# Two gate products of a four-layer convolution kernel, each as one 128x128 product, with sums, bias and relu on VectorE

## The chip, the core and the metric

The kernel runs on one core of a Trainium2 chip. The metric is the device time of one execution in microseconds. The kernel before took 975.81 us (median of three executions, 974.52 to 977.21). A difference under about 0.3%, 2.9 us, can't be told from none.

The core has a matrix engine (TensorE, PE in the profile, with its weight loads as PEld), a vector engine (VectorE, DVE), a scalar engine (ScalarE, ACT), GpSimd (POOL) and SyncE (SP), which issues most transfers. Each works through its own list of instructions in order and waits on semaphores of the others.

## The reference, cut to what matters

Sixteen images of 256 channels, 28 x 28, go through four layers. Layer 1 is the one concerned. It has two branches, each with a gate per image and channel:

```python
def se_gate(mix, w1, b1, w2, b2):
    p = mix.mean(axis=(2, 3))                  # 256 means
    h = jax.nn.relu(p @ w1.T + b1)             # 32 hidden values
    g = jax.nn.sigmoid(h @ w2.T + b2)          # 256 gates
    return g[:, :, None, None]
...
y = prelu(bn(conv3x3(hardsign(x + a_move), a_w), a_bn1), a_alpha2)
mix = s * x + y * (1.0 - s)
y = se_gate(mix, a_se_w1, a_se_b1, a_se_w2, a_se_b2) * y
y = y * residual
y = bn(y, a_bn2) + residual
res2 = y
u = prelu(bn(conv1x1(hardsign(y + f_move), f_w), f_bn1), f_alpha2)
mix2 = s2 * y + (1.0 - s2) * u
u = se_gate(mix2, f_se_w1, f_se_b1, f_se_w2, f_se_b2) * u
return bn(u, f_bn2) + res2
```

So a branch has a product of 256 means with 32 rows, and one of 32 hidden values with 256 rows.

## The kernel before, in words

Layer 0 takes the first 115 us, layer 1 lasts to 479 us, layer 2 to 690 us and layer 3, an attention, to the end.

**An image of layer 1.** Channels lie on 128 partitions in two halves (k for input channels, mo for output channels). `iteration(b)` runs the 3x3 convolution of image b beside the first branch's gate of image b-1 and the second branch's gate of image b-2, so the two gates of one `iteration` share each small product: two columns, one for each branch (g = 0, 1). PE does, in this order: `conv_pair(b, 0, ...)` for parts 1 and 2, then part 0; the product for the hidden sums; part 3; the product for the gates; `conv_pair(b, 1, ...)` for parts 1 and 2, then 0 and 3; and `conv1x1(b - 1)`. That is 96 and 16 matmuls of 392 columns. Their results go to PSUM buffers of `conv_ps`, three of them, six allocations in an image. A buffer is free when its last reader has finished.

**Order by hand.** Layer 1 stands in a `manual_schedule` over PE, DVE and Activation: on these three engines the instructions run in the order of the program text.

**VectorE in an image,** in this order: `enter` (L669) and `prelu_y` (L765) of the next and last image, `unit_b` (L765), three small operations for the means (`hidden_x`, `hidden_a`, L134), `sum_pair_b` (L744), `residual_b` (L705), `transform` (L134, into vs), `residual_b` again, `rows_out` (L753), the product of gates and s_bn (L134 in `gates`), `transform`, `branch1_b` twice (L808), `prelu_y`, `branch2` (L845), `sum_pair_b`, `branch2`, `transform` twice, `rows_out`.

**ScalarE in an image:** `unit_u` (L836), `sign1` (L675), `sum_pair_a` (L734), `residual_a` (L663), `sign1`, the relu in `hidden_b` (L784), `residual_a`, the sigmoid in `gates` (L793), `branch1_a` twice (L801), `widen` (L695), `branch1_c` (L815), `sum_pair_a`, `branch1_c`, `widen`, `squares2` twice (L854), weight passes of layer 2 in images 1 to 12 (L266, L285, L288; L266 in images 1 to 6 only), `widen` twice.

**The gates.** `hidden_sums` (L619) multiplies the means p, 128 x (g, k), with w_1, 128 x (k, 128): two matmuls, k = 0 and 1, add up in PSUM. Of w_1's 128 columns, 32 for each g are filled; the rest is zero. `hidden_b` (L780) adds the bias b_1 and takes the relu with one ScalarE activation for each g, from 32 partitions of PSUM into `hidden`, whose rows 64 and 96 hold a one that brings in the second bias through w_2's rows. `gates` (L787) multiplies w_2, one half mo after the other, takes the sigmoid from PSUM on ScalarE and multiplies with s_bn on VectorE. `gate_bias` (L626) is called in image 0 alone: it adds a constant part of the mean to b_1.

**After the last image** (L990 to L1060) the same functions run twice more in the open: for the last image's first gate, and for its second, whose gate enters the statistics that layer 2's normalization starts from. `keep_busy` puts matmuls without use on PE there. Between the second `hidden_a` and `gates`, program order has `squares2` on ScalarE, `hidden_b`, two `products` (L857) on VectorE, a `squares` (L854), five small VectorE operations, `gates` and another `squares`.

**Loading.** `constants` (L547) works out the small vectors in layer 0 and issues the loads of w_1, w_2 and b_1 on SP. `vec` holds all per-channel vectors, named in `VECS`; `pv` picks one.

Of the kernel before, what the change touches and what calls it, by code (L numbers as in the profile page):

```python
# [27 lines left out]
F32 = mybir.dt.float32  # L28
# [5 lines left out]
AF = mybir.ActivationFunctionType  # L34
ALU = mybir.AluOpType
# [4 lines left out]
P = 128  # L40
# [29 lines left out]
    + [f"a_bn1_{i}" for i in range(4)] + [f"a_bn2_{i}" for i in range(4)]  # L70
    + ["a_scale", "f_move", "f_alpha2"]
    + [f"f_bn1_{i}" for i in range(4)] + [f"f_bn2_{i}" for i in range(4)]
    + ["f_scale", "g1", "b1", "g2", "b2", "g3", "b3", "a1", "a2", "a3"]
)


def conv_seq_kernel(tc: tile.TileContext, d: dict, out: bass.AP):
    again = forward(tc, d, out, False)
    with tc.If(again > 0):
        forward(tc, d, out, True)  # L80
# [3 lines left out]
def forward(ctx: ExitStack, tc: tile.TileContext, d: dict, out: bass.AP, careful: bool):  # L84
# [3 lines left out]
    nc = tc.nc  # L88
    V, A, T = nc.vector, nc.scalar, nc.tensor
# [3 lines left out]
    small = ctx.enter_context(tc.tile_pool(name="small", bufs=3))  # L93
# [7 lines left out]
    def pv(name):  # L101
        return vec[:, VECS.index(name), :]
# [30 lines left out]
    def tt(o, a, b, op):  # L133
        V.tensor_tensor(o, a, b, op)  # L134
        return o

    def rsqrt(name, v, half=None):

        r, t = (const.tile(list(v.shape), F32, name=name + q) for q in ("_r", "_t"))
        A.activation(t, v, AF.Sqrt)  # L140
        V.reciprocal(r, t)
        tt(t, r, r, ALU.mult)
        if half is not None:
            tt(r, r, half, ALU.mult)
        else:
            V.tensor_scalar(r, r, -0.5, None, ALU.mult)
        tt(t, t, v, ALU.mult)
        V.scalar_tensor_tensor(r, t, -3.0, r, ALU.add, ALU.mult)
        return r
# [270 lines left out]
    with tc.tile_pool(name="ps_conv", bufs=3, space=PSUM) as psc, \  # L420
# [13 lines left out]
        with tc.tile_pool(name="ph1", bufs=1) as ph:  # L434
# [104 lines left out]
            ra1, ra2, rf2, us1, ns1 = (vtile(q) for q in ("ra1", "ra2", "rf2", "us1", "ns1"))  # L539
            mix_x, mix_y, mix_c = (const.tile([P, 2, 2], F32, name=n) for n in ("mix_x", "mix_y", "mix_c"))  # L540

            w_1, w_2, b_1 = (ph.tile(sh, F32, name=n) for sh, n in (([P, 2, P], "se1"), ([P, 256], "se2"), ([64, 1], "seb")))

            for t in (w_1, w_2):
                nc.gpsimd.memset(t, 0.0)

            def constants():  # L547
                for p in pads:
                    nc.gpsimd.memset(p, 0.0)
                nc.gpsimd.tensor_copy(  # L550
                    doubts[:, 4 * NB:4 * NB + 6], vec[:, VECS.index("a1"):VECS.index("a3") + 1, :].rearrange("p i k -> p (i k)")
                )
                for i, n in enumerate(("a_alpha2", "f_alpha2")):
                    nc.gpsimd.tensor_copy(doubts[:, 4 * NB + 6 + 2 * i:4 * NB + 8 + 2 * i], pv(n))
                v = const.tile([P, 4, 2], F32, name="v_bn")
                for i, bn in enumerate(bns):
                    V.tensor_scalar(v[:, 2 * i:2 * i + 2], bn[:, 3::4], EPS, None, ALU.add)
                r = rsqrt("bn", v)
                for i, bn in enumerate(bns):
                    two = slice(2 * i, 2 * i + 2)  # L560
                    tt(s_bn[:, two], bn[:, 0::4], r[:, two], ALU.mult)
                    tt(c_bn[:, two], bn[:, 2::4], s_bn[:, two], ALU.mult)
                    tt(c_bn[:, two], bn[:, 1::4], c_bn[:, two], ALU.subtract)
                tt(cc, c2, c4, ALU.add)

                for o, q in ((ra1, "a_alpha1"), (ra2, "a_alpha2"), (rf2, "f_alpha2")):
                    V.tensor_scalar(o, pv(q), -1.0, 1.0, ALU.mult, ALU.add)
                V.tensor_scalar(us1, s1, 1.0 / UP, None, ALU.mult)
                V.tensor_scalar(ns1, s1, -1.0 / UP, None, ALU.mult)
                tt(zb2, c2, pv("f_move"), ALU.add)  # L570
                for g, (q, scale) in enumerate((("a", pv("a_scale")), ("f", pv("f_scale")))):
                    V.tensor_scalar(mix_x[:, g], scale, 1.0 / N, None, ALU.mult)
                    V.tensor_scalar(mix_y[:, g], scale, -1.0 / N, 1.0 / N, ALU.mult, ALU.add)
                    rows = slice(32 * g, 32 * g + 32)
                    nc.sync.dma_start(out=w_1[:, :, rows], in_=d[f"se1_{q}"])
                    nc.sync.dma_start(out=w_2[rows], in_=d[f"se2_{q}"])
                    nc.sync.dma_start(out=b_1[rows], in_=d[f"seb_{q}"])
                    nc.sync.dma_start(out=w_2[64 + 32 * g:65 + 32 * g], in_=d[f"seb2_{q}"])
                tt(mix_c[:, 1], pv("f_scale"), c2, ALU.mult)

            w2a = packed_weights(wpool, tag="wa2")
# [28 lines left out]

            hidden = [ph.tile([P, 2], F32, name=f"hidden{i}") for i in range(3)]
            for t in hidden:
                nc.gpsimd.memset(t, 0.0)
                for g in range(2):
                    nc.gpsimd.memset(t[64 + 32 * g:65 + 32 * g, g:g + 1], 1.0)

            def hidden_sums(p):  # L619

                ps = pss.tile([P, 2], F32, tag="sm", name="hid")
                for k in range(2):
                    T.matmul(ps, lhsT=w_1[:, k, :], rhs=p[:, :, k], start=(k == 0), stop=(k == 1))
                return [ps[32 * g:32 * g + 32, g:g + 1] for g in range(2)]

            def gate_bias():  # L626
                for g, h in enumerate(hidden_sums(mix_c)):
                    rows = slice(32 * g, 32 * g + 32)
                    tt(b_1[rows], h, b_1[rows], ALU.add)

            vs = ph.tile([P, 2, 4, 2, HR, S + 2], FR, tag="vs", name="vs")
            vs16 = vs if careful else ph.tile([P, 2, 4, 2, HR, S + 2], BF16, name="vs16")
# [9 lines left out]
            sums = {}  # L642
# [131 lines left out]
            def hidden_a(t, p):  # L774

                r = small.tile([P, 2, 2], F32, tag="g1", name="g1")
                tt(r, sums_of(t)[1], mix_y, ALU.mult)
                return hidden_sums(tt(p, p, r, ALU.add))

            def hidden_b(t, sums):  # L780
                h = hidden[t % 3]
                for g, ps in enumerate(sums):
                    rows = slice(32 * g, 32 * g + 32)
                    A.activation(h[rows, g:g + 1], ps, AF.Relu, bias=b_1[rows])  # L784
                return h

            def gates(h, f=None):  # L787

                ps = pss.tile([P, 2, 2], F32, tag="sm", name="gate")
                g = small.tile([P, 2, 2], F32, tag="gate", name="gates")  # L790
                for k in range(2):
                    T.matmul(ps[:, k], lhsT=w_2[:, k * P:(k + 1) * P], rhs=h, start=True, stop=True)
                A.activation(g.rearrange("p i k -> p k i"), ps, AF.Sigmoid)  # L793
                if f is not None:
                    return tt(f, g[:, 1], s_bn[:, 3], ALU.mult)
                return tt(g, g, s_bn[:, 1::2], ALU.mult)
# [69 lines left out]
            def iteration(b):  # L866
# [29 lines left out]
                if one:  # L896
                    h = hidden_b(b, h)
# [7 lines left out]
                if one:  # L905
                    g = gates(h)
                else:
                    gate_bias()
# [57 lines left out]
            with tc.manual_schedule(engines={ET.PE, ET.DVE, ET.Activation}):  # L966
# [24 lines left out]
                b = B - 1  # L991
                keep_busy(14)
                g = gates(hidden_b(B, hidden_a(B, px)))
                keep_busy(14)
                branch1_a(b, 1, g[:, 0])
# [33 lines left out]
                h = hidden_a(B + 1, px)  # L1029
                for k in range(2):  # L1030
                    squares2(b - 1, k)
                h = hidden_b(B + 1, h)
                for k in range(2):
                    products(x2[b][:, k, :], shift[:, k:k + 1], us[b, k], sum_uv[:, k:k + 1])
# [4 lines left out]
                tt(v1, v1, sum_vv, ALU.add)  # L1039
                V.tensor_scalar(v1, v1, 1.0 / (B * N), EPS, ALU.mult, ALU.add)  # L1040
                g = gates(h, dqg[:, 2])
                squares(us[b, 1], 0.0, sum_uu[:, 1:2], (B * N)**-0.5)
                keep_busy(14)
# [712 lines left out]
```

## Time and profile before

The profiled execution took 975.5 us; its span from first to last instruction is 973.7 us, at a granted TensorE clock of 0.994.

| from the page and the stretches | value |
|---|---|
| median of three executions | 975.81 us |
| profiled execution, its span | 975.5 us, 973.7 us |
| PE, VectorE, ScalarE busy over the span | 97%, 79%, 74% |
| 130 to 459 us (16 images): PE, VectorE, ScalarE busy | 328.15, 285.18, 265.84 of 329 us |
| 459 to 480 us: the same | 19.21, 17.17, 14.21 of 21 us |
| L623 hidden sums: matmul records, mean | 64 in images 1 to 15, 230 ns |
| L792 gates: the same | 64, 232 ns |
| L784 relu on ScalarE | 32, 252 ns |

A line of a timeline gives start, duration, engine, line of the program, operation, output<-input with shapes, and, in brackets, how long the engine had been idle and what ended it. Several equal instructions in a row are merged (x2). A matmul of 32-bit floats appears as two records. A busy PE is not a PE at its peak, but an engine that never waits sets the pace of its stretch. An operation that also sums up (L669, L765, L808, L845) has a second record of 0.08 us.

### The profile page before, as it was taken

To read this page: it belongs to the slowest core of one execution; us is meant where nothing else is said; L and a number is where in the kernel's file an instruction comes from. 1 tells how busy PE (TensorE), PEld (TensorE's weight loads), DVE (VectorE), ACT (ScalarE), POOL (GpSimd) and SP (SyncE) were. 2 spreads that over 40 slices of the span, in tenths; PEclk is the share of its full clock that TensorE was granted. 3 is DMA by queue.
4 is the path that set the end of the run, shared out by engine and by line. 5 is a ranking of instruction groups with operands and counts; after the bars stand their busy time and mean duration, and the time that the engine had idled before them with its cause. 6 is when DMAs were issued, how large, how long until landed. Compare 5 with 4: busy or idle time off the path is not lost.

```text
span 973.7 us, 14804 instructions
## 1 busy us (share of the span) xinstructions
PE 944.8 (97%) x5615; PEld 582.8 (60%) x5615; DVE 773.4 (79%) x1417; ACT 722.3 (74%) x1199; POOL 141.0 (14%) x149
## 2 busy tenths in 40 slices
PE   7999899999999999999999999999999999999996
PEld 3555568877887878887555555555444444444443
DVE  4767878899998889985799997999757777777765
ACT  6787468888888888874788868887676767666652
POOL 3000100000000000000100000000054444444431
PEclk9999999999999999999999999999999999999998
DMA  9877513334443222110490000000044353525212
GB/s 347 312 271 270 197 50 99 116 115 131 146 152 117 100 100 96 58 63 34 180 383 1 1 1 1 1 1 1 1 71 96 72 129 70 130 67 133 67 67 103
DMA packets 26948, 105.82 MB, mean 109 GB/s; under 512 B 3490, under 2 KB 7268, under 8 KB 26868
## 3 DMA queue, kind: packets, MB, share of 16 engines
q1 hardware_dynamic: 20948, 73.44, 21.2%
q0 software_dynamic: 5632, 30.54, 11.6%
q8 instruction: 46, 0.75, 0.3%
q10 hardware_dynamic: 288, 0.80, 0.2%
q14 instruction: 34, 0.28, 0.1%
HBM read 72.67 MB, written 32.11 MB: 108 GB/s over the span
## 4 chain that ended last, share of the span: by engine, by line
PE 46%; DVE 3%; ACT 1%; issue 1%; DVEq 0%; ACTq 0%
PE cv L340 19%; PE sc L1331 8%; PE av L1352 8%; PE mi L1308 4%; PE sm L1394 2%; PE mi L1412 2%; PE sm L1352 1%; DVE p L1118 1%; DVE ab L354 0%; ACT es L1335 0%; DVE l2b_fin L1120 0%; DVE l2c_fin L1120 0%; DVE r L1378 0%; DVE p L1295 0%; PE sc L1412 0%
## 5 line engine op out<-in xcount | busy, mean ns | idle before, releaser
L340 PE MATMUL cv<-fpads,wpk 128*128 128x392 f16 (+1 forms) x1746 | 295.7, 331 | 10.2 <-ACT fpads L451 5.0
L713 PE MATMUL cv<-vs,w 128*128 128x392 bf16 (+1 forms) x1536 | 287.1, 356 | 2.9 <-DVE vs L134 2.7
L340 PEld LDWEIGHTS <-wpk 128*128 128x128 f16 x1746 | 169.0, 97 | 137.3 <-issue 9.9
L713 PEld LDWEIGHTS cv<-vs,w 128*128 128x128 f32 x768 | 142.6, 190 | 11.7 <-ACT vs L695 0.7
L1335 ACT ACTIVATE es<-sc 128x784 f32<-128x784 f32 x112 | 87.3, 822 | 41.4 <-PE sc L1331 41.4
L713 PEld LDWEIGHTS <-w 128*128 128x128 f16 x768 | 67.7, 101 | 58.1 <-issue 18.5
L1331 PE MATMUL sc<-q,keyswa 64*128 64x392 f32 x448 | 89.9, 513 | 0.9 <-ACT es L1335 0.9
L1118 DVE SCALAR_TENSOR_TENSOR p<-ab,vec 128x392 f32<-128x392 f32 x128 | 79.1, 618 | 2.3
L1352 PE MATMUL av<-es,v 128*64 128x392 f32 x448 | 80.7, 499 | 0.0
L1345 POOL TENSOR_TENSOR sum<-sum,es 128x784 f32<-128x784 f32 x32 | 67.2, 2100 | 3.1 <-ACT es L1335 0.6
L1331 PEld LDWEIGHTS sc<-q,keyswa 64*128 64x128 f32 x448 | 38.9, 186 | 44.0 <-issue 17.1
L851 POOL DMA_DIRECT2D x2d<-x x16 | 8.6, 537 | 343.9 <-DVE x L845 280.9
L1319 DVE COPY keyswa<-mi 64x392 f32<-64x392 f32 x31 | 16.3, 564 | 52.6 <-ACT q L1315 52.5
L1352 PEld LDWEIGHTS av<-es,v 128*64 128x64 f32 x448 | 29.4, 136 | 47.4 <-issue 47.0
L695 ACT CAST vs<-vs 128x840 fp32r<-128x840 bf16 x64 | 54.7, 882 | 1.5 <-DVE vs L134 1.5
L351 ACT ACTIVATE t<-cv,rounding 128x392 f32<-128x392 f32 (+2 forms) x82 | 51.6, 630 | 4.9 <-PE cv L340 1.9
L1123 ACT ACTIVATE t<-ab 128x392 f32<-128x392 f32 x64 | 33.5, 524 | 27.9 <-DVE ab L354 27.9
L823 PE MATMUL cv<-z,fw 128*128 128x392 f32 x256 | 48.9, 342 | 1.0 <-ACT z L815 0.8
L354 DVE SCALAR_TENSOR_TENSOR ab<-ab,cv 128x392 f32<-128x392 f32 x64 | 35.5, 554 | 17.5 <-ACT ab L352 17.5
L823 PEld LDWEIGHTS cv<-z,fw 128*128 128x128 f32 x256 | 45.7, 188 | 2.3 <-ACT z L815 2.1
L1308 PE MATMUL mi<-p,wqk 128*128 128x392 f32 x124 | 45.3, 506 | 0.3 <-DVE p L1295 0.3
L432 PE MATMUL unused<-idle 128*128 128x512 bf16 x175 | 40.5, 389 | 3.0 <-POOL idle L468 3.0
(287 smaller groups left out, 1511.4 us busy)
## 6 DMA issues: line engine op xcount, KB each, us to landing
xs<-in_x_dram SPq DMA_DIRECT2D x30, 784.0 KB, 5.8
x2d<-x POOLq DMA_DIRECT2D x16, 784.0 KB, 3.8
out_dram<-p SPq DMA_DIRECT2D x15, 784.0 KB, 3.8
p<-x2d POOLq DMA_DIRECT2D x14, 784.0 KB, 6.9
p<-x2d SPq DMA_DIRECT2D x13, 784.0 KB, 16.1
n0d<-n POOLq DMA_DIRECT2D x16, 392.0 KB, 4.7
n<-n0d SPq DMA_DIRECT2D x16, 392.0 KB, 3.3
st<-in_w_dram SPq DMA_DIRECT2D x12, 384.0 KB, 6.1
```

The lines of the kernel that those rows point to most:

```text
L340: T.matmul(pss[j][:, n // size if careful else h, :rows * S].rearrange("p (a b) -> p a b", b=S), lhsT=w[:, n, t, :], rhs=pads[:, blocks[j] ...
L351: A.activation(by_halves(t, blocks[j]), ps, AF.Identity, bias=rounding, scale=1.0 / PACK)
L432: tc.keep_in_program_order(T.matmul(ps, lhsT=idle[:, 0:P], rhs=idle, start=True, stop=True))
L695: A.copy(v, w)
L713: T.matmul(ps.rearrange("p (a b) -> p a b", b=S), lhsT=w[:, k, c, u, mo * P:(mo + 1) * P], rhs=v[:, b % 2, u, k, :, c:c + S], start=(n == ...
L823: T.matmul(ps[:, h, :HN], lhsT=w[:, k, mo * P:(mo + 1) * P], rhs=z2[b][:, k, h * HN:(h + 1) * HN], start=(k + i == 0), stop=(k + i == 2),)
L1118: V.scalar_tensor_tensor(p, y, alpha[:, mo:mo + 1], y, ALU.mult, ALU.max)
L1308: T.matmul(ps[:, h, :HN], lhsT=wqk[:, k, :], rhs=x[b][:, k, h * HN:(h + 1) * HN], start=(k == 0), stop=(k == 1))
L1331: T.matmul(ps[:, h, :HN], lhsT=chunk[rows], rhs=qs[b][rows], start=True, stop=True)
L1335: A.activation(e, ps[:, :, :HN], AF.Exp, scale=0.125)
L1345: (V if late else nc.gpsimd).tensor_tensor(sums[b, late], sums[b, late], e, ALU.add)
L1352: T.matmul(ps[64 * h:64 * h + 64, :HN], lhsT=w, rhs=e[:, h, :], start=start, stop=stop)
```

## The change

Both halves k of the means go through one product: w_1 becomes 128 x 128, with 64 columns for k = 0 and 64 for k = 1, and the right side has four columns (g, k). What is wanted are partitions 0 to 63 in columns k = 0 and partitions 64 to 127 in columns k = 1; VectorE adds these two. Both halves mo of the gates also go through one product: w_2 becomes 128 x 128, with 64 rows for each mo, and `hidden` gets four columns (mo, g), in each of which 32 rows are filled. The relu moves to VectorE; the second bias is no longer a row of w_2 but a vector b_2 that VectorE adds ahead of the sigmoid.

```diff
-            w_1, w_2, b_1 = (ph.tile(sh, F32, name=n) for sh, n in (([P, 2, P], "se1"), ([P, 256], "se2"), ([64, 1], "seb")))
-
-            for t in (w_1, w_2):
-                nc.gpsimd.memset(t, 0.0)
+            w_1, w_2, b_1, b_2 = (
+                ph.tile(sh, F32, name=n)
+                for sh, n in (([P, 2, 64], "se1"), ([P, P], "se2"), ([P, 1], "seb"), ([P, 2, 2], "seb2"))
+            )
...
                     nc.sync.dma_start(out=w_1[:, :, rows], in_=d[f"se1_{q}"])
-                    nc.sync.dma_start(out=w_2[rows], in_=d[f"se2_{q}"])
-                    nc.sync.dma_start(out=b_1[rows], in_=d[f"seb_{q}"])
-                    nc.sync.dma_start(out=w_2[64 + 32 * g:65 + 32 * g], in_=d[f"seb2_{q}"])
+                    for mo in range(2):
+                        nc.sync.dma_start(
+                            out=w_2[64 * mo + 32 * g:64 * mo + 32 * g + 32], in_=d[f"se2_{q}"][:, mo * P:(mo + 1) * P]
+                        )
+                    nc.sync.dma_start(out=b_1[64 + 32 * g:96 + 32 * g], in_=d[f"seb_{q}"])
+                    V.tensor_copy(b_2[:, g], pv(f"{q}_se_b2"))
...
-            hidden = [ph.tile([P, 2], F32, name=f"hidden{i}") for i in range(3)]
+            hidden = [ph.tile([P, 2, 2], F32, name=f"hidden{i}") for i in range(3)]
             for t in hidden:
                 nc.gpsimd.memset(t, 0.0)
+
+            def flat(t):
+                return t.rearrange("p i j -> p (i j)")
+
+            def hidden_sums(p):
+
+                ps = pss.tile([P, 2, 2], F32, tag="sm", name="hid")
+                T.matmul(flat(ps), lhsT=flat(w_1), rhs=flat(p), start=True, stop=True)
+                return ps
+
+            def gate_bias():
+                ps = hidden_sums(mix_c)
+                t = small.tile([P, 2], F32, tag="hb", name="hb")
+                V.tensor_copy(t[64:P], ps[0:64, :, 0])
                 for g in range(2):
-                    nc.gpsimd.memset(t[64 + 32 * g:65 + 32 * g, g:g + 1], 1.0)
-
-            def hidden_sums(p):
-
-                ps = pss.tile([P, 2], F32, tag="sm", name="hid")
-                for k in range(2):
-                    T.matmul(ps, lhsT=w_1[:, k, :], rhs=p[:, :, k], start=(k == 0), stop=(k == 1))
-                return [ps[32 * g:32 * g + 32, g:g + 1] for g in range(2)]
-
-            def gate_bias():
-                for g, h in enumerate(hidden_sums(mix_c)):
-                    rows = slice(32 * g, 32 * g + 32)
-                    tt(b_1[rows], h, b_1[rows], ALU.add)
+                    rows = slice(64 + 32 * g, 96 + 32 * g)
+                    V.scalar_tensor_tensor(b_1[rows], ps[rows, g, 1:2], t[rows, g:g + 1], b_1[rows], ALU.add, ALU.add)
...
-            def hidden_b(t, sums):
+            def hidden_b(t, ps):
                 h = hidden[t % 3]
-                for g, ps in enumerate(sums):
+                r = small.tile([64, 2], F32, tag="hb", name="hb")
+                V.tensor_scalar(r, ps[64:P, :, 1], b_1[64:P], None, ALU.add)
+                for g in range(2):
                     rows = slice(32 * g, 32 * g + 32)
-                    A.activation(h[rows, g:g + 1], ps, AF.Relu, bias=b_1[rows])
+                    for mo in range(2):
+                        V.tensor_scalar(
+                            h[64 * mo + 32 * g:64 * mo + 32 * g + 32, mo, g:g + 1], ps[rows, g, 0:1], r[rows, g:g + 1], 0.0,
+                            ALU.add, ALU.max,
+                        )
                 return h

             def gates(h, f=None):

                 ps = pss.tile([P, 2, 2], F32, tag="sm", name="gate")
                 g = small.tile([P, 2, 2], F32, tag="gate", name="gates")
-                for k in range(2):
-                    T.matmul(ps[:, k], lhsT=w_2[:, k * P:(k + 1) * P], rhs=h, start=True, stop=True)
-                A.activation(g.rearrange("p i k -> p k i"), ps, AF.Sigmoid)
+                T.matmul(flat(ps), lhsT=w_2, rhs=flat(h), start=True, stop=True)
+                tt(g, ps.rearrange("p k i -> p i k"), b_2, ALU.add)
+                A.activation(g, g, AF.Sigmoid)
```

Two names, `a_se_b2` and `f_se_b2`, are added to the end of `VECS`, and the arrays `seb2_a` and `seb2_f` go.

## The prediction

> **What bounds the kernel now.** I read the page's engine shares first (PE 97% busy), then the busy time by stretches of one image of layer 1, then the waits and the timeline of layer 1. Three lines of the stretches, all within 134 to 459 us:
>
> ```profile
> 258.60:279.50 20.90, 20.90 (x122) 16.81 (x121) 19.52 (x46) 18.38 (x28) 0.53 (x1) 1.00 0.40 134
> 342.20:363.10 20.90, 20.90 (x122) 16.82 (x121) 18.51 (x39) 17.76 (x27) 0.53 (x1) 1.00 0.34 116
> 425.80:446.70 20.90, 20.90 (x122) 16.81 (x120) 14.58 (x33) 12.52 (x19) 0.64 (x2) 1.00 0.10 40
> ```
>
> The numbers are PE, PEld, VectorE, ScalarE and POOL. PE has no idle time: an image takes 20.92 us because its matmuls take that. But VectorE is at 19.5 where layer-2 weights are signed beside it (images 1 to 6), 18.5 later: 1.4 to 2.4 us of slack. Next, the timeline around image 8's two products:
>
> ```profile
> 287.60 1.15 DVE L753 SCALAR_TENSOR_TENSOR y<-cv,us,uvs 128x392 f32<-128x392 f32 x2
> 289.78 6.68 PE L713 MATMUL cv<-vs,w 128*128 128x392 bf16 x36
> ...
> 295.58 0.62 DVE L744 SCALAR_TENSOR_TENSOR uvs<-cv,ns,t 128x392 f32<-128x392 f32 x1
> 296.12 1.03 DVE L705 SCALAR_TENSOR_TENSOR xs<-rn,ra,xs 128x784 f32<-128x784 f32 x1
> 296.31 0.50 PE L623 MATMUL hid<-g,se 128*128 128x2 f32 x4
> 296.67 2.32 PE L713 MATMUL cv<-vs,w 128*128 128x392 bf16 x12
> 296.85 0.52 ACT L784 ACTIVATE hidden<-hid,seb 32x1 f32<-32x1 f32 x2 [0.15 <-PE hid L623]
> ...
> 298.37 1.04 DVE L705 SCALAR_TENSOR_TENSOR xs<-rn,ra,xs 128x784 f32<-128x784 f32 x1 [0.72 <-ACT rn L663]
> 299.32 1.16 DVE L753 SCALAR_TENSOR_TENSOR y<-cv,us,uvs 128x392 f32<-128x392 f32 x2
> 299.36 0.17 ACT L793 ACTIVATE gates<-gate 128x4 f32<-128x4 f32 x1 [1.02 <-PE gate L792]
> 300.39 0.15 DVE L134 TENSOR_TENSOR gates<-gates,s_bn 128x4 f32<-128x4 f32 x1
> ```
>
> The reader is to see two things. The hidden sums (L623) and their relu (L784) sit on PE and ScalarE; VectorE passes them by and starts L705 0.2 us before PE has even begun them. And the last rows of an image (L753 at 287.60, done at 288.75) are only 1.03 us ahead of the next image's first matmul at 289.78, which needs their PSUM buffer: three buffers, six allocations per image, so allocation 7 takes the buffer of allocation 4. That is the slack to watch.
>
> **What the skill says.** "VectorE: DVE Perf Modes", section on two Vector instructions with no wait between them: an instruction whose input or output starts in another group of 32 partitions than the one before is held until all earlier ones have finished. The trace agrees: the two 32-row additions of L134 into seb take 0.30 us together at 0.15 each, without overlap, while full-height small ones start 0.07 apart (107.04, 107.11, 107.18). "Perfetto Trace Analysis", section on Scalar/DVE operations: per-instruction overhead of about 125 ns for VectorE on PSUM; the trace has 0.136 to 0.151 for those. "TensorE: Matmul & The Clock Gate", specifications table: VectorE and ScalarE queues are strict FIFO, so one waiting instruction stops all behind it. "FP8 and Floating Point Precision", TensorE notes, gives true FP32 four passes; the trace shows two records per matmul (x68 for 34), so I count two.
>
> **PE.** Seen in ever wider windows, the four passes of L623 end 0.28, 0.39, 0.50 us after their start: 0.11 each. Both products halve from four passes to two: 0.22 each, 0.45 per image, 0.22 in image 0 (mix_c only). If PE stayed the bound, 15 x 0.45 + 0.22 = 6.9 us would go.
>
> **VectorE, per image.** Call T the moment it can start hidden_b: end of the second pass plus the 0.04 us seen from PE to ScalarE (296.31 + 0.50 + 0.04 = 296.85), so 296.31 + 0.28 + 0.04 = 296.62, or 6.84 after the image's first matmul (289.78). In program order hidden_b stands after sum_pair_b (L744, ended 296.20) and before L705: VectorE now waits 0.4 us for PE, which it did not.
> hidden_b is five instructions. The first (64 rows from PSUM) 0.15; the next reads its result, and dependent small ones stand 0.035 apart (474.59 + 0.16, next at 474.79). Then four 32-row ones, each in other groups of partitions: 4 x 0.16 = 0.64. Sum 0.84. The trace has no such instruction with a pointer scalar of 32 rows: below, 0.43 if they overlap like the full-height ones; above, 1.15 if each costs the 0.22 of L1023, the one small operation with a pointer scalar. I take 0.84.
> Then, from T: L705 at 0.84, transform at 1.78, L705 at 2.29 (its ScalarE input is early, since the relu left ScalarE's queue), L753 at 3.24, the new addition of b_2 at 4.31 (pitches 0.94, 0.51, 0.95, 1.07 from the timeline; PE's part of each is done). Sigmoid used to run at PE's end, beside L753 (299.36); it now waits for that addition: 0.16 + 0.04, sigmoid 0.17 + 0.04, so the product with s_bn starts at 4.73, with VectorE idle in between. From there as before: 0.19 to ScalarE's L801, 1.08 to L808, then 8.02 without a gap to the end of the last L753 (280.73 to 288.75). End: T + 14.02; next image's matmul at T + 14.08.
> Loop: 6.84 + 14.08 = 20.92 us. That is what PE takes now. So PE's 0.45 comes back as a wait for PSUM ahead of each image: **no gain, no loss, in images 2 and 7 to 14**.
>
> **Images with weight signs.** There a second loop is longer: VectorE's second L845 is at T + 10.90 (it was 4.90 after L808), feeds ScalarE's squares, which are followed without a gap by three or four weight passes, two casts and L836, which VectorE's L765 needs before L744. From L845 (243.78) to the end of L744 (254.40) the trace has 10.62. Loop 10.90 + 10.62 + 0.03 = 21.55, against 20.92: +0.63 for each of five images (2 to 6, up to T of image 7), +0.15 once for sf's tail at 268.4: **+3.3 us**. Before, this loop had slack because the chain from PE to ScalarE took nothing of VectorE. In images 7 to 12 it is 10.90 + 9.90 + 0.03 = 20.83, just covered.
>
> **First and last images.** Images 0 and 1 have no branch 2 on VectorE (1.9 us less), so PE keeps 0.22 + 0.45: **-0.67**. In image 15 VectorE has no next image; addition and sigmoid cost 0.4, two halved products give back 0.2 of it before L801, and PE already waits for ScalarE's z (0.85 us at 451): **+0.19**.
>
> **The tail,** where everything is in the open:
>
> ```profile
> 472.27 1.03 DVE L857 SCALAR_TENSOR_TENSOR product<-x,shift,last 128x784 f32<-128x784 f32 x1
> 473.23 1.03 DVE L857 SCALAR_TENSOR_TENSOR product<-x,shift,last 128x784 f32<-128x784 f32 x1
> ...
> 473.12 0.52 ACT L784 ACTIVATE hidden<-hid,seb 32x1 f32<-32x1 f32 x2 [0.53 <-PE hid L623]
> ...
> 474.64 0.17 ACT L793 ACTIVATE gates<-gate 128x4 f32<-128x4 f32 x1
> 474.71 0.85 ACT L854 ACTIVATE square<-last 128x784 f32<-128x784 f32 x1
> 475.66 1.28 ACT L1045 ACT_TABLE_LOAD   x1
> ```
>
> First gate (461 to 464): relu 0.84 instead of 0.57, addition +0.20, products -0.45: **+0.09**. Second: L857's two products stand behind hidden_b, which waits for PE until 472.90 and ends at 473.75; they go from 472.27 to 473.75, and the five small operations behind them end 1.48 later too, at 476.44. Only then the addition of b_2, then the sigmoid at 476.54, and behind it on ScalarE the last square, which ended at 475.65 and now ends at 477.55: **+1.9**. The table load, root and sign of layer 2's start follow it.
>
> **Costed at nothing:** two copies into b_2 and one more instruction in gate_bias on VectorE (0.2 to 0.5 us in all; layer 0 and image 0 leave it idle); eight small loads on SP as before, in other sizes; some ten POOL memsets less, long before their readers. ScalarE's 0.52 per image freed is inside its waits. Layers 0, 2, 3 only shift. Without that cover, 0.5 us in all.
>
> **Sum:** -0.67 + 3.3 + 0 + 0.19 + 0.09 + 1.9 = +4.8 us, on the profiled execution's 975.5 (span 973.7 and 1.8 around it), which is within 0.3 of the median 975.81: **980.3 us**. With d for the error of hidden_b's 0.84, the time moves by 16 d (13 loops, image 15, two gates).
>
> **Rivals.**
> (1) Not slower: VectorE's detour is short enough for PE to keep its gain. For: held instructions are priced from only two additions. Against: waits for PE and for the sigmoid remain. It decides where hidden_b costs under 0.54 (d = -0.3 cancels the 4.8); at 0.43, 4.8 - 16 x 0.41 = -1.8: 973.7.
> (2) Dear scalars: hidden_b at 1.15, d = +0.3: 985.1. For: L1023's 0.22. Against: that one also waits.
> (3) The signing loop is not binding, as ScalarE, rid of 0.52, runs ahead: 980.3 - 3.3 = 977.0. Against: its squares wait for VectorE.
>
> **How the numbers follow.** Chances: forecast 0.50, rivals 0.20, 0.15, 0.15. A change under 0.3% (2.9 us) can't be told here from none. Rival 3 and most of rival 1 lie within it; faster by more needs d under -0.48, just beyond the lower bound: 0.05. Slower: 0.45 of the forecast, rival 2 and a share of the others' upper edges, 0.70; same 0.25. Range 975.5 to 985.
>
> **What would show it.** Right: gaps on PE of about 0.4 us ahead of each image's first L713, ended by VectorE's L753; larger ones in images 3 to 7; image period 20.9 later, 21.5 there; L705 about 1.3 us later against PE; the sigmoid waiting for VectorE; the last square near 477.5 plus what came before. Wrong: PE without gaps at 20.5 us per image, or hidden_b's five far from 0.84.

## The result and the profile after

The changed kernel takes **986.26 us** (median of 4 runs, 985.93 to 987.82), against 975.30 for the kernel before in the same runs (974.52 to 977.21): a ratio of **1.0113, interval 1.0097 to 1.0129**. It is 1.1% slower, where 980.3 us had been forecast, and lies above the range. The profiled execution took 987.82 us, its span is 986.0. In the two traces layer 2's first matmul starts at 479.07 us before and at 490.48 after: +11.41 us of the 12.3 by which the two spans differ arise ahead of layer 2. From there to the end the twelve traces of this document take between 494.2 and 496.1 us, with 494.7 before and 495.6 after, so below the start of layer 2 is compared as well as the time.

First, busy time by stretches of one image, of the kernel after (columns: stretch, its length, then PE, PEld, VectorE, ScalarE, POOL, TensorE clock, DMA share, GB/s). The first line is an image with weight signs, the second one without, the third has few branches left.

```profile
257.88:280.08 22.20, 20.92 (x118) 16.31 (x117) 20.85 (x51) 17.93 (x27) 0.53 (x1) 1.00 0.39 127
323.48:344.80 21.32, 20.61 (x118) 16.49 (x118) 19.75 (x45) 17.03 (x26) 0.53 (x1) 1.00 0.33 114
430.17:451.50 21.33, 20.60 (x117) 16.48 (x117) 18.03 (x40) 13.27 (x19) 0.64 (x2) 1.00 0.10 39
```

PE was busy for all of its 20.90 us. Now it is busy for 20.6 of 21.33: the halved products are in the first figure, and the second is longer all the same. No engine is full any more. That is the mark of a loop through several engines, each waiting for the next. The view of waits over layer 1 (after) names its links: who waited, for whom, us in total, times, the longest.

```profile
ACT gates L807 <- DVE gates L134: 62.6, 16, 6.4
PE cv L719 <- DVE y L759: 12.6, 13, 1.3
DVE gates L134 <- ACT gates L807: 4.3, 16, 0.3
DVE hb L791 <- PE hid L626: 2.1, 5, 0.5
```

The wait that costs is the second: PE, 13 times, for rows_out's PSUM buffer, 0.97 us on average. The first is large and harmless, since it costs nothing that ScalarE waits there. The fourth, VectorE waiting for PE ahead of hidden_b, came only five times: in images 1, 2, 14 and 15 and after the last. The timeline after, from the last rows before image 8 to the product with s_bn:

```profile
294.44 1.16 DVE L759 SCALAR_TENSOR_TENSOR y<-cv,us,uvs 128x392 f32<-128x392 f32 x2
295.65 6.64 PE L719 MATMUL cv<-vs,w 128*128 128x392 bf16 x36 [1.26 <-DVE y L759]
...
302.13 0.28 PE L626 MATMUL hid<-g,se 128*128 128x4 f32 x2
302.27 2.33 PE L719 MATMUL cv<-vs,w 128*128 128x392 bf16 x12
302.45 0.23 DVE L791 TENSOR_SCALAR hb<-hid,seb 64x2 f32<-64x2 f32 x1
302.71 0.89 DVE L795 TENSOR_SCALAR hidden<-hid,hb 32x1 f32<-32x1 f32 x4
303.63 1.03 DVE L711 SCALAR_TENSOR_TENSOR xs<-rn,ra,xs 128x784 f32<-128x784 f32 x1
...
306.13 1.16 DVE L759 SCALAR_TENSOR_TENSOR y<-cv,us,uvs 128x392 f32<-128x392 f32 x2
307.21 0.15 DVE L134 TENSOR_TENSOR gates<-gate,seb 128x4 f32<-128x4 f32 x1
307.40 0.20 ACT L807 ACTIVATE gates<-gates 128x4 f32<-128x4 f32 x1 [3.66 <-DVE gates L134]
307.63 0.16 DVE L134 TENSOR_TENSOR gates<-gates,s_bn 128x4 f32<-128x4 f32 x1 [0.27 <-ACT gates L807]
```

PE begins image 8 0.05 us after L759 has released the buffer, having waited 1.26 us. The product takes two passes (0.28) instead of four (0.50). VectorE then spends 302.45 to 303.63, **1.18 us**, on hidden_b's five instructions before residual_b (L711) may start; before, it started L705 0.2 us ahead of the product. After L759 come the addition of b_2, the sigmoid and the product with s_bn, one after another. Everything of the loop that the forecast named is there; hidden_b is longer than it was priced.

The tail, after:

```profile
482.11 0.89 DVE L795 TENSOR_SCALAR hidden<-hid,hb 32x1 f32<-32x1 f32 x4
483.02 1.03 DVE L871 SCALAR_TENSOR_TENSOR product<-x,shift,last 128x784 f32<-128x784 f32 x1
...
485.74 0.16 DVE L134 TENSOR_TENSOR gates<-gate,seb 128x4 f32<-128x4 f32 x1
485.94 0.21 ACT L807 ACTIVATE gates<-gates 128x4 f32<-128x4 f32 x1 [0.89 <-DVE gates L134]
486.05 0.84 ACT L868 ACTIVATE square<-last 128x784 f32<-128x784 f32 x1
487.00 1.28 ACT L1059 ACT_TABLE_LOAD   x1
```

The products (L871) stand behind hidden_b, the addition of b_2 behind them, and the last square and the table load behind the sigmoid.

The ledger, by the starts of each image's first convolution and of the tail's products:

| part | forecast | of it with 0.34 more per hidden_b | measured |
|---|---|---|---|
| up to image 2 (images 0 and 1) | -0.67 | -0.67 | -0.77 |
| images 2 to 7 (weight signs) | +3.3 | +5.3 | +6.6 |
| images 8 to 14 | 0 | +2.4 | +2.9 |
| image 15 | +0.19 | +0.53 | -0.25 |
| first gate of the tail | +0.09 | +0.43 | +0.47 |
| second gate to layer 2 | +1.9 | +2.24 | +2.46 |
| sum | +4.8 | +10.2 | +11.4 |

The 0.34 is 1.18 less the forecast's 0.84. The first row says little: image 2 starts anywhere between 162.7 and 165.4 us in the twelve traces, and not in the order of what PE has to do. An image took 20.92 us throughout; it now takes 21.33, and 22.05 to 22.2 where weights are signed.

### The profile page after: what moved, and what is told of

It is laid out like the page before. It is cut to its first block, busy times and chain, and to the rows that moved or that the text cites. A ratio compares the mean times of both kernels' runs of the same rounds, so it can differ in the third digit from the quotient of the medians.

```text
span 986.0 us, 14732 instructions
## 1 busy us (share of the span) xinstructions
PE 941.3 (95%) x5539; PEld 575.7 (58%) x5545; DVE 795.7 (81%) x1522; ACT 712.1 (72%) x1165; POOL 139.6 (14%) x141
## 3 DMA queue, kind: packets, MB, share of 16 engines
q0 software_dynamic: 5632, 30.55, 11.4%
## 4 chain that ended last, share of the span: by engine, by line
PE 45%; DVE 4%; ACT 1%; issue 1%; DVEq 0%; ACTq 0%
PE cv L340 19%; PE sc L1345 8%; PE av L1366 8%; PE mi L1322 4%; PE sm L1408 2%; PE mi L1426 2%; PE sm L1366 1%; DVE p L1132 1%; DVE r L1392 1%; DVE ab L354 0%; DVE l2c_fin L1134 0%; DVE l2b_fin L1134 0%; DVE p L1309 0%; DVE p L1308 0%; PE sc L1366 0%
## 5 line engine op out<-in xcount | busy, mean ns | idle before, releaser
L340 PE MATMUL cv<-fpads,wpk 128*128 128x392 f16 (+1 forms) x1746 | 297.5, 332 | 11.3 <-ACT fpads L451 5.3
L340 PEld LDWEIGHTS <-wpk 128*128 128x128 f16 x1746 | 169.5, 98 | 140.2 <-issue 12.2
L719 PEld LDWEIGHTS cv<-vs,w 128*128 128x128 f32 x768 | 142.8, 191 | 11.4 <-ACT vs L701 0.7
L807 ACT ACTIVATE gates<-gates 128x4 f32<-128x4 f32 x17 | 3.5, 205 | 63.5 <-DVE gates L134 63.5
```

Source lines behind the costliest of these rows:

```text
L340: T.matmul(pss[j][:, n // size if careful else h, :rows * S].rearrange("p (a b) -> p a b", b=S), lhsT=w[:, n, t, :], rhs=pads[:, blocks[j] ...
L719: T.matmul(ps.rearrange("p (a b) -> p a b", b=S), lhsT=w[:, k, c, u, mo * P:(mo + 1) * P], rhs=v[:, b % 2, u, k, :, c:c + S], start=(n == ...
```

## The experiments

Four questions: why hidden_b takes 1.18 (the first two runs), what the tail's order is worth, whether the sigmoid's detour costs what was said, and where the work ought to stand. Differences are against the changed kernel, in the last part against the one before. Every ratio is to the kernel before.

### Is it the pointer scalar, or the change of partitions?

**Immediates in place of the pointer scalars.**

```diff
-                V.tensor_scalar(r, ps[64:P, :, 1], b_1[64:P], None, ALU.add)
+                V.tensor_scalar(r, ps[64:P, :, 1], 0.0, None, ALU.add)
...
-                            h[64 * mo + 32 * g:64 * mo + 32 * g + 32, mo, g:g + 1], ps[rows, g, 0:1], r[rows, g:g + 1], 0.0,
+                            h[64 * mo + 32 * g:64 * mo + 32 * g + 32, mo, g:g + 1], ps[rows, g, 0:1], 0.0, 0.0,
```

> Left out: the second half of the hidden sums and the bias (the five VectorE instructions of hidden_b take the constant 0.0 where they took a column of b_1 or r), so it isn't the reference's gate; instructions, partitions and order are the changed kernel's. Theory A, the per-partition scalar is what makes each of them 0.21 us instead of the 0.15 of a 32-row addition: hidden_b falls from 1.18 to about 0.85, the image period from 21.33 to about 21.0, the time from 986.3 by 16 x 0.33 to about 981. Theory B, moving between groups of 32 partitions is what costs: hidden_b stays at 1.1 to 1.2, the time at 986.

**All four on partitions 0 to 31.**

```diff
-                            h[64 * mo + 32 * g:64 * mo + 32 * g + 32, mo, g:g + 1], ps[rows, g, 0:1], r[rows, g:g + 1], 0.0,
+                            h[0:32, mo, g:g + 1], ps[0:32, g, 0:1], r[0:32, g:g + 1], 0.0,
```

> Left out: three of the four blocks of the hidden values (all four 32-row instructions of hidden_b read and write partitions 0 to 31); their scalars stay. Theory A, the scalar costs and partitions don't matter: four instructions keep their distance of 0.22, hidden_b 1.18, time 986. Theory B, each is held until the one before has finished because it starts in another group of partitions: three of the four come closer, 0.08 to 0.1 apart, hidden_b about 0.75 to 0.8, image period about 20.9, time about 986.3 - 16 x 0.4 = 980. Both can be true; then the distance falls to something between, and hidden_b to 0.9 to 1.0.

The instructions of hidden_b in the three kernels, from the view of one tile (duration in ns: least, median, most; first and last start). After:

```profile
L791 DVE TENSOR_SCALAR hb<-hid,seb x17: 223/224/225, 149.8 to 481.8; 64x2 f32<-64x2 f32 x17
L795 DVE TENSOR_SCALAR hidden<-hid,hb x68: 204/210/215, 150.1 to 482.8; 32x1 f32<-32x1 f32 x68
```

With immediates:

```profile
L795 DVE TENSOR_SCALAR hidden<-hid x68: 145/150/155, 150.3 to 478.5; 32x1 f32<-32x1 f32 x68
```

On the same rows:

```profile
L795 DVE TENSOR_SCALAR hidden<-hid,hb x68: 195/196/207, 150.7 to 475.8; 32x1 f32<-32x1 f32 x68
```

And in the timeline, with immediates:

```profile
300.96 0.16 DVE L791 TENSOR_SCALAR hb<-hid 64x2 f32<-64x2 f32 x1
301.14 0.64 DVE L795 TENSOR_SCALAR hidden<-hid 32x1 f32<-32x1 f32 x4
301.81 1.04 DVE L711 SCALAR_TENSOR_TENSOR xs<-rn,ra,xs 128x784 f32<-128x784 f32 x1
```

and on the same rows:

```profile
320.65 0.23 DVE L791 TENSOR_SCALAR hb<-hid,seb 64x2 f32<-64x2 f32 x1
320.91 0.58 DVE L795 TENSOR_SCALAR hidden<-hid,hb 32x1 f32<-32x1 f32 x4
321.42 1.01 DVE L711 SCALAR_TENSOR_TENSOR xs<-rn,ra,xs 128x784 f32<-128x784 f32 x1
```

Both are at work, and the two views show them apart. A pointer scalar makes each of these instructions 0.06 us longer (0.210 against 0.150; 0.224 against 0.16 for the 64-row one): without it hidden_b takes 300.96 to 301.81, 0.85 us, which is the forecast's 0.84. On the same rows the four are still 0.196 long, yet start 0.13 apart, because they overlap; with changing rows they start 0.225 apart, each after the end of the one before. That is what the Trainium skill, "VectorE: DVE Perf Modes", says in its section on two Vector instructions with no wait between them; here it costs 0.095 us for each of the four. Without it hidden_b is 0.77.

| | hidden_b | image | image with signs | layer 2 starts | median, us | ratio (interval) |
|---|---|---|---|---|---|---|
| after | 1.18 | 21.33 | 22.06 | 490.48 | 986.26 | 1.0113 (1.0097 to 1.0129) |
| immediates | 0.85 | 21.03 | 21.75 | 486.18 | 983.67 | 1.0086 (1.0065 to 1.0106) |
| same rows | 0.77 | 20.80 | 21.53 | 483.25 | 981.13 | 1.0059 (1.0039 to 1.0078) |

What is taken off hidden_b comes off each image: 0.33 shorter gives 0.30, 0.41 shorter gives 0.53. The 0.12 more in the second case is mostly a second hold, further down: L759, the first instruction behind hidden_b that reads PSUM again, starts 1.04 us after the second L711 in the changed kernel and 1.06 with immediates, only when L711 has ended, but 0.95 on the same rows, before that, as in the kernel before. PE does the same matmuls in all three. So VectorE's list sets the loop. Images with signs stay 0.73 above the others in all three. The times, 983.67 and 981.13, fell less than expected (about 981 and 980).

### The tail's order

The products go ahead of hidden_b, and the last square ahead of the sigmoid.

```diff
-                h = hidden_b(B + 1, h)
                 for k in range(2):
                     products(x2[b][:, k, :], shift[:, k:k + 1], us[b, k], sum_uv[:, k:k + 1])
+                h = hidden_b(B + 1, h)
...
-                g = gates(h, dqg[:, 2])
                 squares(us[b, 1], 0.0, sum_uu[:, 1:2], (B * N)**-0.5)
+                g = gates(h, dqg[:, 2])
```

> The changed kernel with the order after the last image altered: the two products of the variance stand ahead of hidden_b on VectorE, and the last square ahead of the sigmoid on ScalarE. Theory, the second gate's operations in the open cost what the order makes them wait: the first small operation of layer 2's normalization comes about 1.4 us earlier, time about 984.9. Rival, layer 2's start waits for something else (the sign buffers, its loads): unchanged, 986.3.

It took 985.65 us (985.16 to 987.42), ratio 1.0108 (1.0087 to 1.0129), where 984.9 had been expected; the 0.6 less than after can't be told from none. Counted from the start of the last L626 (480.69 here, 481.50 after; that lead is older than the edited lines), the table load starts 4.10 us later instead of 5.50, and the sign of layer 2's first input (L1098) 6.99 instead of 8.18. So the chain has gained 1.2 to 1.4 us. But layer 2's first matmul comes 9.25 us later instead of 8.98. PE sat longer at the gate's product, and what it does next slowed. PE in this run:

```profile
483.73 0.36 PE L805 MATMUL gate<-hidden,se 128*128 128x4 f32 x2 [2.73 <-DVE hidden L795]
483.94 6.16 PE L432 MATMUL unused<-idle 128*128 128x512 bf16 x20
489.94 1.35 PE L340 MATMUL cv<-fpads,wpk 128*128 128x392 f16 x7
```

and after:

```profile
483.35 4.48 PE L432 MATMUL unused<-idle 128*128 128x512 bf16 x20
490.48 1.81 PE L340 MATMUL cv<-fpads,wpk 128*128 128x392 f16 x5 [2.65 <-ACT fpads L1098]
```

Busy times of short stretches give the reason, with the granted clock behind the five engines; the first line is this run, the second, in a fence of its own, is after, 5 us later:

```profile
485.00:488.00 3.00, 3.00 (x8) 1.07 (x7) 2.70 (x15) 1.80 (x4) 1.34 (x3) 0.50 0.74 243
```

```profile
490.00:492.00 2.00, 1.52 (x5) 0.72 (x6) 1.35 (x4) 2.00 (x4) 0.35 (x1) 0.50 1.04 427
```

In this run PE waited 2.73 us for hidden_b, and TensorE was then granted half its clock for 3.41 us. That fell on the 20 filler matmuls (L432), which took 6.16 us instead of 4.48. Layer 2's first matmul stood behind them and came 2.26 us after the start of L1098 (487.68), where it comes 0.80 after it in the changed kernel.

The changed kernel has the same half clock, later: PE waits 2.65 us for L1098, and the 3.41 us fall on layer 2's first matmuls. From the first of L340 to the twenty-first it takes 4.78 us, against 3.40 in this run and 3.51 in the kernel before, where PE waits only 0.43 at that place. So by its twenty-first matmul this order is 1.1 us ahead after all (12.65 us behind L626, against 13.76). The loss of clock has moved, and most of what the chain gains is left, too little to show in these times.

Around the start of layer 2, the half clock follows PE's waits of 2.39 us (same rows), 2.65 (after and immediates) and 2.73 in the twelve traces, and none of the others there, which are 2.08 or less. The Trainium skill, "TensorE: Matmul & The Clock Gate", Part 1, has the half rate after at least one idle window of about 3.4 us, in windows that run on whatever the kernel does; here waits shorter than that were enough.

### The sigmoid's detour

Four sigmoids with b_2 as bias on ScalarE, straight from PSUM, without the addition on VectorE.

```diff
-                tt(g, ps.rearrange("p k i -> p i k"), b_2, ALU.add)
-                A.activation(g, g, AF.Sigmoid)
+                for k in range(2):
+                    for i in range(2):
+                        A.activation(g[:, i, k:k + 1], ps[:, k, i:i + 1], AF.Sigmoid, bias=b_2[:, i, k:k + 1])
```

> The changed kernel with b_2 added by ScalarE: four sigmoids of one column each with the bias, in place of VectorE's addition and one sigmoid. hidden_b stays on VectorE. Theory, each image pays 0.42 us for the addition and for VectorE waiting out the sigmoid behind it, and four sigmoids are done before VectorE gets to the product with s_bn: image period 21.33 to 20.91, time 986.3 - 14 x 0.42 = about 980.5. Rival, the addition hides beside other work and only hidden_b counts: period 21.3, 986.

981.29 us (980.11 to 981.97), ratio 1.0055 (1.0037 to 1.0073); an image takes 20.89 us, where 20.91 was expected. Its timeline:

```profile
303.76 0.71 ACT L808 ACTIVATE gates<-gate,seb 128x1 f32<-128x1 f32 x4 [1.07 <-PE gate L805]
305.14 1.16 DVE L759 SCALAR_TENSOR_TENSOR y<-cv,us,uvs 128x392 f32<-128x392 f32 x2
306.21 0.15 DVE L134 TENSOR_TENSOR gates<-gates,s_bn 128x4 f32<-128x4 f32 x1
```

The sigmoids run beside L759, and the product with s_bn follows it at once. The four take 0.71 us where one took 0.20, and that costs nothing, because ScalarE has to wait for the product with s_bn afterwards in any case. The forecast's 0.42 for addition and sigmoid fits: 21.33 - 20.89 = 0.44.

### hidden_b on ScalarE

The five as ScalarE activations, the addition of b_2 left on VectorE.

```diff
-                V.tensor_scalar(r, ps[64:P, :, 1], b_1[64:P], None, ALU.add)
+                A.activation(r, ps[64:P, :, 1], AF.Identity, bias=b_1[64:P])
...
-                        V.tensor_scalar(
-                            h[64 * mo + 32 * g:64 * mo + 32 * g + 32, mo, g:g + 1], ps[rows, g, 0:1], r[rows, g:g + 1], 0.0,
-                            ALU.add, ALU.max,
+                        A.activation(
+                            h[64 * mo + 32 * g:64 * mo + 32 * g + 32, mo, g:g + 1], ps[rows, g, 0:1], AF.Relu,
+                            bias=r[rows, g:g + 1],
```

> The changed kernel with hidden_b's five instructions on ScalarE (one addition of 64 rows, four rectifications of 32), the addition of b_2 still on VectorE. Theory, VectorE's 1.18 us go, but ScalarE's next residual now waits for 1.3 us of small instructions and VectorE's second residual for that, so only about 0.33 per image comes back: period 21.0, time about 981.8. Rival, the whole 1.18 comes back and PE sets the pace again: period 20.5, time below 975.

Neither: 987.36 us (986.73 to 988.72), ratio 1.0126 (1.0108 to 1.0144), an image takes 21.42. The timeline, ScalarE's lines and one of VectorE's:

```profile
302.98 0.95 ACT L681 ACTIVATE pad<-xs,zb 128x784 bf16<-128x784 f32 x1
303.95 0.26 ACT L791 ACTIVATE hb<-hid,seb 64x2 f32<-64x2 f32 x1
304.24 1.04 ACT L795 ACTIVATE hidden<-hid,hb 32x1 f32<-32x1 f32 x4
305.31 0.95 ACT L669 ACTIVATE rn<-xs,nbi 128x784 f32<-128x784 f32 x1
...
306.30 1.03 DVE L711 SCALAR_TENSOR_TENSOR xs<-rn,ra,xs 128x784 f32<-128x784 f32 x1 [1.41 <-ACT rn L669]
```

ScalarE comes to the product only 0.5 us after PE has ended it (303.45), behind L681, then spends 1.33 us on the five; rn (L669) is late by that, and VectorE's second L711 waits 1.41 us for it, against 0.72 before the change. Moved to the other engine, the same delay reaches VectorE through rn.

### A part of the change alone, and the weight signs moved

**Only the first product halved**, its sum and relu by three ScalarE instructions, one more than before; the gates as before.

```diff
-                for k in range(2):
-                    T.matmul(ps, lhsT=w_1[:, k, :], rhs=p[:, :, k], start=(k == 0), stop=(k == 1))
+                T.matmul(flat(ps), lhsT=flat(w_1), rhs=flat(p), start=True, stop=True)
...
+                r = small.tile([64, 2], F32, tag="hb", name="hb")
+                A.activation(r, ps[64:P, :, 1], AF.Identity, bias=b_1[64:P])
...
-                    A.activation(h[rows, g:g + 1], ps, AF.Relu, bias=b_1[rows])
+                    A.activation(h[rows, g:g + 1], ps[rows, g, 0:1], AF.Relu, bias=r[rows, g:g + 1])
```

> The first product of the change alone, off VectorE: w_1 as one 128 x 128 product, its two halves added and rectified by three ScalarE instructions (0.25 each, about 0.83 in all, where two took 0.53), the gates' product, bias row and sigmoid as in the kernel before. Theory, the loss is VectorE's detour and PE keeps what doesn't wait: PE stays without gaps, each of 16 images loses two passes of 0.11, about 3.5 us in all, period 20.7, time about 972. Rival, ScalarE's later residual pushes VectorE's chain past its 1 us of slack: PE waits ahead of each image, 975 to 977.

973.76 us (972.88 to 975.63) against 974.87, ratio 0.9985 (0.9978 to 0.9992); about 972 had been expected. A later image takes 20.70 us and is PE alone, 0.22 less, as two passes should give; an image with signs has 21.13, more than before; PE waits for 0.16 of it and counts as busy for the rest:

```profile
212.00:233.10 21.10, 20.94 (x120) 16.54 (x118) 18.87 (x41) 18.61 (x30) 0.53 (x1) 1.00 0.41 132
...
316.60:337.30 20.70, 20.70 (x120) 16.64 (x119) 18.55 (x39) 18.03 (x29) 0.53 (x1) 1.00 0.33 117
```

**The same, with layer 2's weight signs (images 1 to 6) moved** to ScalarE's pause behind the sigmoid, from the end of its list of an image.

```diff
+                lates = [s.work() for s in early[b]]
...
-                lates = [s.work() for s in aside[b][::-1]]
+                lates += [s.work() for s in aside[b][::-1] if s not in early[b]]
```

> e4_scalar_sum with the weight signs of images 1 to 6 on ScalarE moved from behind the squares to the idle time behind the sigmoid. In e4 images 3 to 7 had 20.9 to 21.2 us, the others 20.7. Theory, in those images the loop of VectorE and ScalarE through the squares, the weight passes and the casts sets the pace, and 0.74 leaves it: all images at 20.7, time 973.8 - 2 = about 971.9. Rival, something else binds there (a load, the PSUM buffers): 973.8.

> e8_sum_and_signs once more, beside e10_signs_alone and the kernel before on one chip: period 20.7 in all images, 2 to 4 us faster than before.

972.98 us (970.09 to 975.75), ratio 0.9968 (0.9953 to 0.9983), and in a second run beside other kernels 973.04, ratio 0.9970 (0.9957 to 0.9982), where about 971.9 had been expected. PE is now the whole of every image, those with signs too; layer 2 starts at 476.45 in the second:

```profile
212.56:233.27 20.71, 20.71 (x120) 16.64 (x119) 18.96 (x40) 18.74 (x30) 0.53 (x1) 1.00 0.40 136
...
295.40:316.10 20.70, 20.70 (x121) 16.63 (x120) 18.52 (x39) 18.01 (x29) 0.53 (x1) 1.00 0.34 117
```

**The move alone**, on the kernel before:

> The kernel before with nothing but the weight signs moved as in e8_sum_and_signs. Theory, there PE sets the pace in all images, so ScalarE's order is of no account and e8's gain is the halved first product's: period 20.92, time 975. Rival, the move itself is what gained in e8: about 973.

976.70 us against 976.04, ratio 1.0007 (0.9998 to 1.0017), an image takes 20.92: where PE fills an image, taking the signs away from behind it brings nothing. The gain of the version above is the shorter PE list, and the move only lets it through.

**Both products halved, all small work on ScalarE, signs moved.** This is the whole aim of the change without a single instruction more on VectorE in an image.

> Both products as in the changed kernel, but everything around them on ScalarE: hidden_b as in e6, sigmoids as in e5, and the weight signs moved as in e8. VectorE does what it did before the change. Theory, VectorE's chain ends 0.75 earlier than in the changed kernel (21.33 to 20.58), close to what PE needs with four passes less (20.48); period 20.5 to 20.6, about 1 us lost after the last image where nothing covers ScalarE's small instructions: time about 970.7. Rival, ScalarE, now with eight small instructions more per image, sets the pace: above 975.

976.89 us against 974.88, ratio 1.0014 (1.0003 to 1.0026), where 970.7 had been expected: an image takes 20.92, not 20.58. Its waits:

```profile
DVE xs L713 <- ACT rn L671: 19.6, 14, 1.5
...
PE cv L721 <- DVE y L761: 3.9, 12, 0.4
```

As in the run with hidden_b on ScalarE, rn is late (1.4 us an image), and PE waits 0.33 us for the buffer in 12 images. With all nine small instructions on ScalarE the kernel still comes out no faster than before.

## Why the forecast was wrong in size

**Right.** PE's part: two passes less for each product, 0.11 each. From image 8 on hidden_b starts 0.04 to 0.06 us after the product's end; 0.04 was taken. PE's gain comes back as waits for rows_out's PSUM buffer ahead of each image. Images with weight signs are longer than the rest. Addition and sigmoid cost 0.42 in series. In the tail the table load is late because products, addition and sigmoid are queued behind one another. The step "a loop through VectorE to the buffer's release, and not PE, sets the image" is shown by the two hidden_b experiments: PE's work unchanged, the image shorter.

**The term that was mis-sized: hidden_b.** The forecast put it at 0.84: 0.15 for the first, then "four 32-row ones, each in other groups of partitions: 4 x 0.16 = 0.64". It took these durations from small operations without a pointer scalar and put the nearest one that had it, the 0.22 of L1023, aside with "that one also waits". The trace of the kernel before doesn't bear that out:

```profile
470.53 0.16 DVE L1022 SCALAR_TENSOR_TENSOR l_d<-shift,sx 128x2 f32<-128x2 f32 x1
470.72 0.22 DVE L1023 SCALAR_TENSOR_TENSOR svv<-l_d,shift,svv 128x1 f32<-128x1 f32 x1
```

L1023 starts 0.04 us after L1022 has ended, which is the distance that the forecast itself took for dependent small operations, so that wait lies ahead of its 0.22 and not in it; L1022, without a pointer scalar, takes 0.16. The missing 0.06 stood there. Measured for hidden_b are 0.224 and four times 0.225, 1.18 with the gaps. That the four are held was right; that the pointer scalar costs 0.06 us apiece was missing, and with immediates the sum is 0.85. By the forecast's own "16 d", d = 0.34 is +5.4 us: 4.8 + 5.4 = 10.2, of 11.4 measured. Rival 2, "dear scalars", gave 985.1 us from hidden_b at 1.15, and is what happened; its chance of 0.15 and the range, which ended at 985, were too small for a price whose nearest row in the trace was the upper one.

**Smaller errors.** The step from the second L711 to L759 was taken as 0.95, as before, and is 1.04 in every image from 2 on. The forecast applied the hold by partitions to the four small instructions alone; the experiment on the same rows, in which the step is 0.95 again, shows that they hold L759 as well. Later images lose 0.41 instead of 0.34: 0.09 more by this step, and 0.04 less because the product comes 6.80 us after the image's first matmul and not 6.84.

The wait of 0.4 us for PE ahead of hidden_b is there only in images 2, 14 and 15. In images 3 to 7 VectorE gets there 0.6 us after the product's end, which fits the forecast's second loop, through ScalarE. In images 8 to 13 it gets there within 0.03 us of the product's end, so that both loops seem to take about 21.33 there; the traces don't tell which of them leads.

In images 3 to 7 the excess over the later ones is 0.73 (0.89 in image 7, where the forecast had 0.15 for sf's tail) and not 0.63, and image 2, which was not counted, has 0.39 more than those. Why stays open.

Image 15 was forecast as a loss of 0.19 and is a gain of 0.25. There VectorE waits 1.03 us for PE ahead of L759, so hidden_b is covered; and ScalarE no longer waits 0.31 for PE at L740 (L734 before), which had made its second z late. Images with signs, later images and image 15 together are +1.0 of the 1.2 us that hidden_b leaves open.

Layers 2 and 3 were taken to shift only. In the profiled execution layer 2's first twenty matmuls cost 1.3 us more than before (4.78 against 3.51), by the half clock behind PE's wait of 2.65 us.

**The other rivals.** Rival 1 (not slower) fails at the same price. With hidden_b at 0.77 an image without signs is already shorter than before (20.80), but those with signs (21.53) and the tail keep the kernel slower. Rival 3, that the signs' loop doesn't bind, is refuted by the 22.06; and with only the first product halved, moving the signs takes the excess away (21.13 to 20.70).

## What to carry to other kernels

Price a small instruction from a row with the same form of operands: of 0.225 us here, 0.06 is the pointer scalar and 0.095 the start in another group of partitions. Then look for the instruction further down that the change of partitions holds as well (0.09 here). Before a consumer moves to an engine that works in order, follow the loop from its new place to the buffer that it releases; a slack of 1 us is soon spent, though the engine is idle for 2 us in each round.

Of the versions tried, only those that halve the first product alone, with three small instructions on ScalarE, were faster than before: by 0.15%, and by 0.3% once the signs no longer stand behind. That is at the edge of what can be told from none; the shorter images in the traces speak for it more than the times. The second product alone was not run.

## What was not expected of the hardware

- A pointer scalar lengthens a VectorE instruction of 32 rows and one column from 0.150 to 0.210 us, and one of 64 rows and two columns from 0.16 to 0.224.
- Held by a change of partitions, such instructions start 0.225 us apart; not held, 0.13, though each is 0.196 long. The next instruction that read PSUM, a long one further down, was held with them: it started 1.04 us after the one before it, instead of 0.95.
- PE waits of 2.39 to 2.73 us were followed by 3.41 us at a granted clock of 0.50, in which 20 filler matmuls took 6.16 us instead of 4.48. Waits of 2.08 us and less around the start of layer 2 were not.
- Four sigmoids of 128x1 with a bias take 0.71 us on ScalarE where one of 128x4 takes 0.20, and with them, and no addition on VectorE, an image of this kernel is 0.44 us shorter.
